# Moving weight loads around the last cross-attention section of a fused decoder kernel

## Chip, core and metric

The kernel runs on one core of one Trainium2 chip. The metric is device time in microseconds (us) of one launch, as the median of several runs. The kernel before the change has a median of 1155.73 us over three runs (1155.29 to 1156.04).

## The reference, cut to what matters

Sixteen sequences of 128 rows and 512 columns go through one decoder layer and then through a gated cross-attention layer, all in float32.

```python
# decoder layer
x = x + attention(layernorm(x, ln1) @ w_qkv + b_qkv, ltor_mask) @ w_ao + b_ao          # self attention, 16 heads of 32
x = x + attention(layernorm(x, ln2) @ w_q + b_q, ctx @ w_kv + b_kv, cross_mask) @ w_co + b_co
x = x + gelu(layernorm(x, ln3) @ w1 + b1) @ w2 + b2                                     # 512 -> 2048 -> 512
# gated layer: keys and values come from the same ctx
a = layernorm(ctx, gamma, beta)
x = x + tanh(gate) * (attention(x @ Wq.T, a @ Wk.T, a @ Wv.T, mask) @ Wo.T)
```

## The kernel before

**Sections and steps.** The sixteen sequences form four groups of four. The decoder's attention is eight sections in a row: A0 to A3 (self attention of each group) and B0 to B3 (cross attention of each group). A section has sixteen steps, numbered 0 to 15, four for each sequence (called a batch here); the last section, B3, is followed by eight steps of run-out, numbered 16 to 23. In every step the function `attend` lets each engine do a little of several pipelines: the scores of a batch at steps 0, 4, 8 and 12; the exponentials, sums and scaling of one unit (four heads) per step; and what other sections need later. The order of all instructions is written out by hand and kept (`keep_in_program_order`). Each engine works through its own list in that order.

**How probabilities reach TensorE.** After scaling, a unit's probabilities are transposed on VectorE and stored to DRAM (`away_B <- s_B`, 256 KB). Two units later they are fetched as a pair in four parts (`pT_B <- away_B`, 4 x 128 KB) into one of three `pT` buffers. Then TensorE mixes them with the values (`av_B <- pT_B, v_B`) and projects (`mo_B`). For B3 the pairs are fetched at steps 7 and 9 for the first batch (mixed at step 12), 11 and 13 for the second (step 15), 14 and 16 for the third (step 18), 18 and 20 for the fourth (step 22).

**One queue for transfers.** Nearly all DMAs are issued by SyncE (SP in the profile) in the written order. They use eight semaphores in turn, so a DMA cannot be issued before the one eight places ahead of it has landed.

**What else runs beside B2 and B3.** While B2 runs, `FirstGated.prepare` normalizes the gated layer's first group (`back_a`, `T_a`) and loads the transposed key weight `w_gk` in steps 8 to 11 and the value weight `w_gv` in steps 12 to 15, in four parts of 256 KB each; they were written to DRAM much earlier. While B3 runs, `beside_last_cross` projects that group's keys (steps 1, 2, 3, 5) and values (7, 9, 13, 15) and prepares the MLP: it normalizes group 0 and sends it turned through DRAM (`turned_C`, then `back_C`, four parts at steps 7, 7, 9, 9), and it fetches rows of `x` that lay in DRAM (`x <- kept_x_B`, steps 1, 1, 3).

**The MLP.** It is a generator (`mlp`) that is advanced by one `piece` at the listed steps. It works in sixteen stages n of seven rounds r; stage 0 begins at step 17 of B3. Stage n needs a block of w1 and a block of w2 (1 MB each, `w1_n` and `w2_n`, both plainly `w` in the profile) and sums of their quarters (`t`). In the first group the sums are stored to DRAM for reuse (`kept <- t`, 1 MB each). The parts of `w1_0` are loaded in steps 12 to 15 of B2. The eight 256 KB parts of `w2_0` and then `w1_1` are queued in `ml.pieces` and issued at the steps in `loads`. In stage 0 VectorE takes two jobs per round from `todo`: the sums of `w2_0` (`first`), then those of `w1_1` and the store of these (`more`). The sums of `w1_0` are stored at the end of round 3.

The rounds fall on the steps as follows: n = 0 has r = 0 at step 17, r = 1 at 18, r = 2 and 3 at 19, r = 4 at 20, r = 5 and 6 at 21; n = 1 begins at step 22. A `piece` begins with `due()`, which issues what the pieces before it left for later, such as a store.

**Weight buffers.** All weights share six buffers (`wpool`, tag `w`). A new tile takes a buffer that is free by the written order, and its load waits until the last reader of the old tile is done.

Of the kernel before, what the change touches and what calls it, by code (L numbers as in the profile page):

```python
# [16 lines left out]
P = 128  # L17
# [3 lines left out]
NQ = S // Q  # L21
# [33 lines left out]
def decoder_then_gated_cross_attention(ctx: ExitStack, tc: tile.TileContext, a: dict, out: bass.AP):  # L55
# [945 lines left out]
    class CrossAttention(Section):  # L1001
# [34 lines left out]
        def jobs(self):  # L1036
            g, n, lnT, encT = self.g, self.name, self.lnT, self.encT
            mask = work.tile([P, 2, GB, S], F32, tag="mask", name=f"mask_{g}", bufs=2)
            self.ms, self.ma = mask[:, 0], mask[:, 1]
            nc.sync.dma_start(  # L1040
                out=self.ms, in_=a["mask_Bx1xSxS2_ff1"][g * GB : (g + 1) * GB, 0].rearrange("b q k -> q b k")
            )
            qkv_tiles(self)
            tokens_at = [x[g][:, b].rearrange("p (o t) -> p o t", t=HF) for b in range(3)]
            token_sides, sums = right_blocks(encT, tokens_at)
            if g == 0:
                self.begin()
            products = [
                block_product(halves(self.k), self.k_sides, token_sides, False, f"k_{n}", ("b_k", 0)),
                block_product(by_quarters(self.v), self.v_sides, token_sides, True, f"v_{n}"),  # L1050
            ]
            return plan(
                ([lambda c=c: self.query_chunk(c) for c in range(KC)], [0, 1, 3, 5]),
                *blocks_plan(products, CROSS_BLOCKS if g else FIRST_CROSS_BLOCKS), ([lambda: mask_terms(self.ms, self.ma)], [7]),
                ([lambda o=o: nc.gpsimd.tensor_tensor(*o) for o in sums], [0, 1, 2, 3]),
                *(self.weights_begin() if g == 0 else decoder[NG + g - 1].tokens_again([5, 9, 13])),
            )

        def query_chunk(self, c):
# [81 lines left out]
    def mlp_start(ml):  # L1141

        ml.b2 = load_row(a["L0_xattn_b2"], "b2_row")
        ml.db1 = cpool.tile([P, NF], F32, tag="db1", name="db1")
        for i in range(NI):
            b1, c0 = columns["b1"]
            c0 += i * KC
            nc.vector.tensor_tensor(
                ml.db1[:, 2 * i : 2 * i + 2], b1[:, c0 + 2 : c0 + 4], b1[:, c0 : c0 + 2], ALU.subtract
            )  # L1150

        def row_difference():
            ml.db2 = work.tile([P, H], F32, tag="row", name="db2_row", bufs=2)
            nc.vector.tensor_tensor(ml.db2[:, 0:HF], ml.b2[:, HF:H], ml.b2[:, 0:HF], ALU.subtract)

        ml.lnT = []
        def start():
            ml.lnT.append(act_tile("C0"))
            ml_begin(0)

        sends = [lambda b=b: ml_send(0, b) for b in range(GB)]
        back = [lambda k=k: chunk_back(ml.lnT[0][:, k], ml.back, k, "ln3_s", "ln3_b") for k in range(KC)]
        return (
            ([start, row_difference, lambda: ml_receive(0)], [0, 5, 7]), (sends, [0, 1, 2, 3]), (back, [12, 13, 14, 14]),
            ([lambda m=m: ml.part(m) for m in range(NQ)], [7, 7, 9, 9])
        )

    def ml_begin(g):
# [8 lines left out]
    def mlp(ml, last_steps):  # L1177
# [145 lines left out]

        w1[0] = load(0, 1)
        yield
        w2[0], w1[1] = load(0, 2), load(1, 1)
        right1[0], todo, _ = sums(0, 1, "enc", w1.pop(0), nc.gpsimd)
        yield
        for do in todo:
# [7 lines left out]
        for n in range(len(steps) + 1):  # L1337
            todo, more = deque(), []
            at_ = {r: [] for r in range(7)}
            h = lnT = None  # L1340
            if n + 1 < len(steps):
                right1[n + 1], more, back = sums(n + 1, 1, "v", w1.pop(n + 1))
                at_[3].append(back)
            if n < len(steps):
                g, i = steps[n]
                right2[n], first, back = sums(n, 2, "enc", w2.pop(n))
                todo.extend(first + more)
                at_[4].append(back)
                h = work.tile([P, KC, TG], F32, tag="qT", name=f"h_{n}", bufs=2)
                if i == 0 and n:  # L1350
                    sides = following
                if g + 1 < NG and i == 1:
                    at_[0].append(lambda: ml_begin(g + 1))
                    for b in range(GB):
                        at_[b].append(lambda b=b: ml_send(g + 1, b))
                elif g + 1 < NG and i == 2:
                    lnT = turned_tile(g + 1)
                    at_[0].append(lambda: ml_receive(g + 1))
                    for m in range(NQ):
                        at_[m // 2].append(lambda m=m: ml.part(m))  # L1360
                    for c in range(KC):
                        at_[3 + c].append(
                            lambda c=c: chunk_back(lnT[c // 2][:, c % 2], ml.back, c, "ln3_s", "ln3_b")
                        )
                    next_lnT = lnT
                elif g + 1 < NG and i == 3:
                    following, more = sums_of(g + 1, next_lnT)
                    for r, do in enumerate(more):
                        at_[3 + r].append(do)
            if before is not None:  # L1370
                for r, do in enumerate(before[1]):
                    at_[r].append(do)
            for r in range(7):
                if n < len(steps):
                    p = H_ORDER[r]
                    hidden_product(n, p, sides[p], right1[n][p], h)
                if before is not None:
                    p = O_ORDER[r]
                    out_product(n - 1, p, before[0][p], right2[n - 1][p], acc)
                for _ in range(min(2, len(todo))):  # L1380
                    todo.popleft()()
                for do in at_[r]:
                    if do is not None:
                        do()
                if r == 1 and n + 1 < len(steps):
                    w2[n + 1] = load(n + 1, 2)
                elif r == 2 and n + 2 < len(steps):
                    w1[n + 2] = load(n + 2, 1)
                last_steps(n, r)
                if (n, r) in ((0, 3), (1, 3)):  # L1390
                    d, t = unkept.pop(0)
                    nc.sync.dma_start(out=d, in_=t)
                yield
            if n < len(steps):
                t = work.tile([P, 3, 2, HF], F32, tag="kT", name=f"sh_{n}", bufs=2)
                before = token_sums(halves(h), t[:, 0], t[:, 1], t[:, 2])
# [59 lines left out]

    class FirstGated:


        def prepare(self, p):  # L1460
            if p == 0:
                self.raw = work.tile([P, GB, H], F32, tag="enc", name="enc_D0", bufs=2)
                self.ln, self.away = ln_tile("D0"), away_tile("D0")
            if p in (0, 1):
                for b in (2 * p, 2 * p + 1):
                    nc.sync.dma_start(out=self.raw[:, b, :], in_=a["ctx_2048"][b])
            elif p >= 2 * GB:
                key, k = ("gk", "gv")[p // GB - 2], p % GB
                if k == 0:
                    w[key] = wpool.tile([P, KC, H], F32, tag="w", name=f"w_{key}")  # L1470
                nc.sync.dma_start(out=w[key][:, k], in_=gated[key][:, k])
            if 2 <= p < 6:
                q = p - 2
                normalize_and_send(self.raw[:, q, :], self.ln[:, q], self.away, "D0", q)
            if p >= 12:
                if p == 12:
                    next(in_mlp)
                ml.pieces.popleft()()
            if p in (9, 11):
                if p == 9:  # L1480
                    self.back, self.part = receiver("a0", self.away)
                for m in range(2):
                    self.part(m + 2 * (p == 11))
            if p >= 12:
                if p == 12:
                    self.aT = act_tile("a0", "enc")
                group_back(self.aT, self.back, "gamma", "beta", [p - 12])
# [232 lines left out]
    def beside_last_cross():  # L1720
        flip[0], in_blocks[0] = 2, False
        def piece():
# [1 line left out]
            next(in_mlp)  # L1724

        at_ = [2, 3, 4, 5, 6, 15, 15, 16, 16, 17, 18, 19, 19, 20, 21, 21, 22, 23, 23]
        loads = [5, 7, 9, 11, 13, 14, 15, 16]
        return plan(
            *gated_start(first), *mlp_start(ml), *decoder[-1].tokens_again([1, 1, 3], (1, 0, 2)), ([piece] * len(at_), at_),
            ([lambda: ml.pieces.popleft()()] * len(loads), loads),  # L1730
        )

# [94 lines left out]
```

## Time and profile before

| what | value |
|---|---|
| median of 3 runs | 1155.73 us |
| the profiled execution's own time | 1154.62 us |
| its span (first to last instruction) | 1152.8 us |
| TensorE (PE) busy in the span | 1129.9 us |
| mean granted TensorE clock | 0.997 |
| DMA traffic | 259.81 MB, mean 225 GB/s |
| DMA busy share and rate, 443 to 477 us | 1.04, 277 GB/s |
| the same, 508 to 531 us | 0.99, 269 GB/s |
| scores of B3's batches (`sc_B`), start | 465.34, 481.38, 494.00, 506.35 us |
| first MLP product (`h`), start | 519.88 us |

Every instruction is recorded under one line, L51, which is the helper that keeps the order, so rows are told apart by their tiles: `out <- in`. Buffer numbers are left out, so `w` is any block of w1 or w2 and `t` any of their sums. The scores mark the steps: step 0 of B3 begins at about 465 us, step 4 at 481, step 8 at 494, step 12 at 502 (its mix comes ahead of the scores), step 16 at 519. An idle time in brackets stands before an instruction with the releaser that ended it. The granted clock is the share of full speed that TensorE was given. SP rows are issues of DMAs; the transfer itself runs later.

### The profile page before, as it was taken

The page shows a single profiled execution, that of the slowest core. Times are in us where ns is not written, and L with a number is a line of the kernel's source. Part 1 is how long each engine was busy: PE and PEld are TensorE (multiplying, and loading weights), DVE is VectorE, ACT ScalarE, POOL GpSimd, SP SyncE. Part 2 cuts the span into 40 slices and gives each one's busy share as a digit, 9 for nine tenths or more (in the row PEclk, how much of TensorE's full clock was granted, in tenths as well). Part 3 has the DMA queues.
Part 4 walks back from the last instruction along what each step waited for, and adds up shares of the span by engine and source line. Part 5 has one row for each costly group of instructions (what it writes and reads, how often), then busy time and mean ns, then how long its engine had stood idle before and what let it go on. Part 6 is the DMA issues. An engine that isn't in the chain of part 4 may idle for free.

```text
span 1152.8 us, 22191 instructions
## 1 busy us (share of the span) xinstructions
PE 1129.9 (98%) x7246; PEld 873.1 (76%) x7246; DVE 743.4 (64%) x1919; ACT 611.1 (53%) x2142; POOL 694.6 (60%) x633
## 2 busy tenths in 40 slices
PE   9999999999999999999999999999999999999998
PEld 8877777666675757546788888888888877878875
DVE  6678978798787776987564634443342237767754
ACT  3567676767667666774231333233222337877663
POOL 6798888788868685773333414443342168545873
PEclk9999999999999999999999999999999999999999
DMA  6588889999888879999696696697447827888975
GB/s 222 159 211 233 217 221 224 256 240 260 210 225 217 233 217 250 289 285 294 226 258 234 183 283 191 201 274 261 155 154 228 261 59 201 236 253 230 267 220 175
DMA packets 325284, 259.81 MB, mean 225 GB/s; under 512 B 83560, under 2 KB 280624, under 8 KB 320304
## 3 DMA queue, kind: packets, MB, share of 16 engines
q1 hardware_dynamic: 325128, 258.38, 78.8%
q8 instruction: 58, 0.95, 0.4%
q14 instruction: 58, 0.48, 0.1%
q10 hardware_dynamic: 40, 0.01, 0.0%
HBM read 163.94 MB, written 94.37 MB: 224 GB/s over the span
## 4 chain that ended last, share of the span: by engine, by line
PE 71%; DMA 10%; POOL 6%; DVE 5%; ACT 3%; issue 3%; SPq 2%; POOLq 0%; DVEq 0%; ACTq 0%
PE h L51 17%; PE o L51 16%; PE mo_A L51 4%; PE mm_q_B L51 3%; PE mm_v_B L51 3%; PE mo_B L51 3%; PE mm_v_A L51 3%; PE mm_q_A L51 3%; PE mm_v_D L51 3%; PE mm_k_A L51 3%; PE mm_k_B L51 3%; PE mm_q_D L51 2%; DMA away_D<-s_D 2%; POOL x L51 2%; SPq L51 2%
## 5 line engine op out<-in xcount | busy, mean ns | idle before, releaser
L51 DVE TENSOR_TENSOR h<-h,h 128x512 f32<-128x512 f32 x80 | 54.9, 686 | 114.5 <-PE h L51 114.5
L51 ACT ACTIVATE h<-h 128x512 f32<-128x512 f32 x64 | 40.3, 630 | 161.5 <-DVE h L51 161.5
L51 ACT ACTIVATE s_A<-s_A,mn_A 128x128 f32<-128x128 f32 x256 | 99.4, 391 | 46.7 <-issue 24.1
L51 ACT ACTIVATE s_B<-s_B,mn_B 128x128 f32<-128x128 f32 x256 | 99.4, 392 | 31.1 <-issue 18.2
L51 POOL TENSOR_TENSOR s_D<-s_D,sum_D 128x512 f32<-128x512 f32 x64 | 66.5, 1040 | 57.7 <-DVE sum_D L51 52.2
L51 ACT ACTIVATE s_D<-s_D,mn_D 128x128 f32<-128x128 f32 x256 | 99.1, 392 | 0.4 <-issue 0.4
L51 POOL TENSOR_TENSOR s_B<-s_B,sum_B 128x512 f32<-128x512 f32 x64 | 67.1, 1048 | 52.2 <-DVE sum_B L51 38.1
L51 POOL TENSOR_TENSOR s_A<-s_A,sum_A 128x512 f32<-128x512 f32 x64 | 66.7, 1042 | 30.5 <-DVE sum_A L51 23.9
L51 POOL TENSOR_TENSOR s_A<-s_A,ma 128x512 f32<-128x512 f32 x64 | 81.9, 1280 | 5.1 <-DVE s_A L51 4.1
L51 POOL TENSOR_TENSOR s_B<-s_B,mask 128x512 f32<-128x512 f32 x60 | 76.6, 1277 | 2.2 <-DVE s_B L51 1.3
L51 POOL TENSOR_TENSOR rstd_aD<-rstd_aD,mhalf 128x1 f32<-128x1 f32 x12 | 6.6, 550 | 115.1 <-DVE rstd_aD L51 101.6
L51 POOL TENSOR_TENSOR sh<-h 128x512 f32<-128x512 f32 x32 | 40.6, 1270 | 50.6 <-ACT h L51 49.6
L51 PE MATMUL h<-sx,t 128*128 128x256 f32 x256 | 61.9, 386 | 2.0 <-ACT h L51 2.0
L51 PE MATMUL h<-T_C,w 128*128 128x256 f32 x256 | 61.1, 381 | 0.8 <-DVE h L51 0.8
L51 PE MATMUL h<-T_C,t 128*128 128x256 f32 x256 | 60.6, 379 | 1.0 <-DVE h L51 1.0
L51 PE MATMUL o<-w,h 128*128 128x256 f32 x256 | 60.9, 381 | 0.0
L51 PE MATMUL o<-t,h 128*128 128x256 f32 x256 | 60.5, 379 | 0.0
L51 PE MATMUL o<-t,sh 128*128 128x256 f32 x256 | 60.5, 379 | 0.0
L51 DVE CUSTOM_DVE_ANT_0 s_D<-sc_D,gmask 128x128 f32<-128x128 f32 x256 | 57.2, 283 | 2.1 <-DMA turned_x<-x_D 1.2
L51 PE MATMUL mo_B<-w_co,mT_B 128*128 128x512 f32 x128 | 57.6, 593 | 0.0
L51 PE MATMUL mo_A<-w_ao,mT_A 128*128 128x512 f32 x128 | 57.5, 592 | 0.0
L51 PE MATMUL mm_q_B<-T_B,w_cq 128*128 128x512 f32 x128 | 57.4, 596 | 0.0
(335 smaller groups left out, 3002.0 us busy)
## 6 DMA issues: line engine op xcount, KB each, us to landing
t<-kept SPq DMA_DIRECT2D x24, 1024.0 KB, 8.0
away_A<-s_A SPq DMA_DIRECT2D x64, 256.0 KB, 3.1
pT_A<-away_A SPq DMA_DIRECT2D x128, 128.0 KB, 3.5
away_B<-s_B SPq DMA_DIRECT2D x64, 256.0 KB, 4.5
pT_B<-away_B SPq DMA_DIRECT2D x128, 128.0 KB, 3.7
away_D<-s_D SPq DMA_DIRECT2D x60, 256.0 KB, 3.5
pT_D<-away_D SPq DMA_DIRECT2D x120, 128.0 KB, 2.7
w<-in_L_xattn_w_dram SPq DMA_DIRECT2D x24, 512.0 KB, 6.1
```

Of the source, the lines that this page charges most:

```text
L51: return lambda *args, **kw: self.tc.keep_in_program_order(call(*args, **kw))
```

## The change

- `w_gk` is loaded in steps 14, 14, 15, 15 of B1 in place of steps 8 to 11 of B2; `w_gv` in steps 6 to 9 of B2 in place of 12 to 15.
- `w1_1` comes before `w2_0` in the queue of parts: its parts are issued in steps 2, 3, 4, 5 of B3, those of `w2_0` in steps 13, 15, 16, 17. Before, `w2_0` went at 5, 7, 9, 11 and `w1_1` at 13, 14, 15, 16.
- In stage 0 of the MLP the sums of `w1_1`, with their store, come ahead of those of `w2_0`.
- The last two parts of `back_C` are fetched at step 8 in place of 9; the three rows of `x` at steps 2, 4, 5 in place of 1, 1, 3.

```diff
@@ CrossAttention.jobs
                 *(self.weights_begin() if g == 0 else decoder[NG + g - 1].tokens_again([5, 9, 13])),
+                *(
+                    [([lambda k=k: first.fetch_weight_part("gk", k) for k in range(KC)], [14, 14, 15, 15])]
+                    if g == 2 else []
+                ),
@@ mlp_start
-            ([lambda m=m: ml.part(m) for m in range(NQ)], [7, 7, 9, 9])
+            ([lambda m=m: ml.part(m) for m in range(NQ)], [7, 7, 8, 8])
@@ mlp
-        w2[0], w1[1] = load(0, 2), load(1, 1)
+        w1[1], w2[0] = load(1, 1), load(0, 2)
...
-                todo.extend(first + more)
+                todo.extend(first + more if n else more + first)
@@ FirstGated
+        def fetch_weight_part(self, key, k):
+            if k == 0:
+                w[key] = wpool.tile([P, KC, H], F32, tag="w", name=f"w_{key}")
+            nc.sync.dma_start(out=w[key][:, k], in_=gated[key][:, k])
...
-            elif p >= 2 * GB:
-                key, k = ("gk", "gv")[p // GB - 2], p % GB
-                if k == 0:
-                    w[key] = wpool.tile([P, KC, H], F32, tag="w", name=f"w_{key}")
-                nc.sync.dma_start(out=w[key][:, k], in_=gated[key][:, k])
+            elif 6 <= p < 10:
+                self.fetch_weight_part("gv", p - 6)
@@ beside_last_cross
-        loads = [5, 7, 9, 11, 13, 14, 15, 16]
+        loads = [2, 3, 4, 5, 13, 15, 16, 17]
...
-            *gated_start(first), *mlp_start(ml), *decoder[-1].tokens_again([1, 1, 3], (1, 0, 2)), ([piece] * len(at_), at_),
+            *gated_start(first), *mlp_start(ml), *decoder[-1].tokens_again([2, 4, 5]), ([piece] * len(at_), at_),
```

## The prediction, made before the changed kernel was run

> **What bounds the kernel now.** I read the first part of the page, then who waited for whom on TensorE around B3, its timeline there, the clock in single stretches, and last SP's issues.
>
> ```profile
> PE 1129.9 (98%) x7246; PEld 873.1 (76%) x7246; DVE 743.4 (64%) x1919; ACT 611.1 (53%) x2142; POOL 694.6 (60%) x633
> ```
>
> TensorE is the bound. A change of load times can only act on its idle time, 22.9 us in all, and on the slow stretches behind it. From 400 to 570 us, around everything that the change moves, TensorE waited for this:
>
> ```profile
> PE av_B L51 <- DMA pT_B<-away_B: 2.5, 2, 1.9
> PE h L51 <- ACT h L51: 2.0, 1, 2.0
> PE h L51 <- DVE h L51: 1.8, 2, 1.0
> PE mm_k_B L51 <- ACT q_B L51: 0.6, 1, 0.6
> ```
>
> Only the first row hangs on a transfer: the mixes of steps 12 and 18 waited for fetched probabilities. The `h` rows are the MLP's chain through ACT and DVE.
>
> ```profile
> 504.71 1.71 PE L51 MATMUL av_B<-pT_B,v_B 128*32 128x128 f32 x28 [1.91 <-DMA pT_B<-away_B]
> 506.35 2.09 PE L51 MATMUL sc_B<-k_B,q_B 32*128 32x128 f32 x32
> ...
> 528.00 1.07 PE L51 MATMUL av_B<-pT_B,v_B 128*32 128x128 f32 x28 [0.63 <-DMA pT_B<-away_B]
> ...
> 543.95 1.89 PE L51 MATMUL o<-w,h 128*128 128x256 f32 x8
> 545.77 1.08 PE L51 MATMUL av_B<-pT_B,v_B 128*32 128x128 f32 x32
> 548.84 3.32 PE L51 MATMUL h<-sx,t 128*128 128x256 f32 x8 [1.99 <-ACT h L51]
> ```
>
> The 1.91 us cost more than themselves. Undisturbed, 32 mixes take 1.01 us to the next instruction (480.37 to 481.38) and 32 scores 1.11 (to 482.49). Here 28 mixes took 1.64, which is 0.76 over 28/32 of 1.01, and the scores 2.02, 0.91 over. So this wait is worth 1.91 + 0.76 + 0.91 = 3.6 us. The mix of step 22, at 545.77, did not wait.
>
> ```profile
> 504.70:508.40 3.70, 3.69 (x61) 3.09 (x61) 2.98 (x6) 2.83 (x15) 3.30 (x4) 0.54 1.10 296
> 548.80:552.00 3.20, 3.16 (x9) 2.53 (x10) 2.48 (x4) 0.69 (x1) 0.00 (x0) 0.59 0.25 70
> 565.00:569.00 4.00, 3.44 (x16) 3.05 (x17) 2.72 (x5) 1.65 (x3) 0.93 (x1) 1.00 1.05 354
> ```
>
> The last three columns are granted clock, DMA share and GB/s. After idle times of 1.91 and 1.99 us the clock was 0.54 and 0.59; after 0.98 us (before 565.56) it stayed 1.00.
>
> ```profile
> 494.01 0.91 SPq L51 DMA_DIRECT2D back_C<-turned_C  x2
> 495.25 0.36 SPq L51 DMA_DIRECT2D w<-in_L_xattn_w_dram  x1
> 495.73 1.96 SPq L51 DMA_DIRECT2D away_B<-s_B  x2
> 497.78 2.13 SPq L51 DMA_DIRECT2D pT_B<-away_B  x4
> 500.78 1.02 SPq L51 DMA_DIRECT2D back_C<-turned_C  x2
> ...
> 532.44 0.51 SPq L51 DMA_DIRECT2D w<-in_L_xattn_w_dram  x1
> 532.99 1.16 SPq L51 DMA_DIRECT2D kept<-t  x1
> 538.36 2.21 SPq L51 DMA_DIRECT2D pT_B<-away_B  x4
> 540.66 0.44 SPq L51 DMA_DIRECT2D kept<-t  x1
> ```
>
> Two places to see. The fetch of step 9 (497.78) has two `back_C` parts and one weight part ahead of it and two `back_C` parts behind. The fetch of step 20 (538.36) has one 1 MB store ahead of it and the store of the `w1_1` sums (540.66) behind.
>
> The landing records of the trace show that transfers line up: they land in the order of issue. At step 9 the fetch's last part landed at 504.58, 0.13 us ahead of its mix. At step 20 the landings were `w1_2` 540.86, `kept` 543.47, the fetch's last part 545.59. TensorE was free for that mix at 545.77, so the slack was 545.77 - 545.59 - 0.13 = 0.05 us.
>
> **The change, part by part.**
>
> *Gated weights sooner.* 1 MB each leaves steps 8 to 11 and 12 to 15 of B2. Buffers are free: `w_ao` is last read in A3's projections, before 294 us, and `w_cq` at 426.87 us, before step 6. Where they go, pairs land 7 us or more ahead of their mixes (the fetch of step 5 in B2 ends its issue at 423.3 for a mix at 433.85), which covers four parts at some 0.75 us each; uncovered it would be 3 us. What is gained: at step 12 of B2, ACT waited 1.29 us for `back_a` (455.97), and DVE, busy without a break from 458.4 to 480.9, and POOL, busy without one from 480.9 to 497.5, stood behind it. So the probabilities of step 9 leave up to 1.3 us sooner.
>
> *`w1_1` and `x` rows.* By the landings, a 256 KB transfer takes some 0.7 us of the line. After 477 us, when transfers landed in 2.4 to 2.9 us and nothing stood in line, and ahead of the fetch of step 9, stood two weight parts (steps 5 and 7) and one row (3). Now three parts (3, 4, 5) and two rows (4, 5) stand there: one of each more, 1.4 us.
>
> *`back_C` at 8.* Two parts more ahead of the same fetch. The pair at 500.78 added 2.3 us to the line (505.01 to 507.28). Nothing waited for `back_C` at step 12 (no such row in ACT's waits), so its earlier landing gains nothing.
>
> Sum at step 12: 1.4 + 2.3 - 1.3 = +2.4 us if the line was full from 477 us on. It moved 292 GB/s from 477 to 495 us and 331 from 531 to 546, so 39 GB/s x 18 us = 0.70 MB, or 2.1 us at 331 GB/s, may have been spare. Small packets do not reach that rate; I take two thirds, 1.4. That leaves **+1.0 us**, bounds -3.6 (the wait gone) and +2.4.
>
> *Step 18.* Its fetch loses the weight part of step 14, which had landed before. I take **-0.2**, bounds -0.6 (the wait gone) and +0.7 (one part more).
>
> *Order in stage 0.* TensorE needs neither block's sums before stage 1, so the sums cost nothing by themselves; if `w2_0` landed too late, DVE would wait up to 0.7 us for its last part. But the store of `w1_1`'s sums moves with them. Before, it was the ninth job, taken in round 4 (step 20) and issued at step 21, behind the fetch of step 20. Now it is the fifth, taken in round 2 and issued by the second `piece` of step 19, ahead of the other store and of the fetch. 1 MB took 2.6 us of the line (540.86 to 543.47). The fetch lands 2.6 us later, slack 0.05, so the mix of step 22 waits 2.55. At half clock its 32 matmuls take 0.76 x 32/28 = 0.87 more. Behind it wait ACT's `mT_B`, then ACT's `h`, then TensorE at 548.84, whose slow stretch was there before. Together **+3.4 us**. Below: 0, if the line has room. Above: one more weight part (step 17), 0.7, and 1 MB at 331 GB/s, 3.2: 2.55 + 0.6 + 0.7 + 0.9 = 4.8. DVE waits too: its sums at 543.49 waited for the first store's landing (1.4 us), now 2.6 us later; that runs beside the same delay.
>
> [...]
>
> Sum: 1.0 - 0.2 + 3.4 = +4.2 us. The profiled execution took 1154.62 us around a span of 1152.8; it becomes 1158.8. The median of the runs is 1.11 above it: 1155.73 + 4.2 = **1159.9**.
>
> **Rivals.**
>
> *The line has room, faster.* Transfers overlap instead of lining up, at 531 us as at 497, so neither the parts nor the store push the fetches back, and the 2 MB that left B2 let the fetch of step 9 come in time. Then 3.6 + 0.6 go and nothing comes: 1151.5. For it: latency was down to 2.4 us near 477 us. Against: landings in order, a share near 1. It decides from the point where the last part of step 9 lands 1.9 us sooner and the 1 MB costs the fetch of step 20 under 0.3 us.
>
> *Both, no change.* The first wait goes (-3.6, -0.2) and the store's wait comes (+3.4): 1155.3. For it: the 1.3 us and the spare rate at their best.
>
> *All in a full line.* +2.4 + 0.7 + 4.8 = +7.9: 1163.6; the upper end of my own case.
>
> That the loads do not really come sooner would need a buffer or data held; both are free, as shown.
>
> **How the numbers follow.** A measurement of this kernel tells 0.2% (2.3 us) from no change. My case, slower, has 0.60, from 1158.1 (the store's wait without its clock, 2.55 - 0.2) to 1163.0; no change 0.19; faster 0.21, since ACT, busy without a break from 508.6 to 517.6, would eat part of that gain: 1151.5 to 1153.4. The range leaves out half of the faster case and the tip of mine: 1152.5 to 1162.8.
>
> **What would show it.** Right: a wait of some 2.5 us before the mix of step 22 on `pT_B <- away_B`, with a clock near 0.55 behind it; two `kept <- t` issues in a row ahead of a fetch; the wait of step 12 still there, 2 to 4 us. Wrong: no wait at step 22, or none at step 12, or a new one at steps 0 to 8 of B2, where the gated loads now stand.

## The result, and the profile after

Measured beside the kernel before on the same chip, the changed kernel took 1161.55 us (median of 8 runs, 1158.16 to 1165.94) against 1155.51 (8 runs, 1154.23 to 1158.61): a ratio of 1.0056 [1.0040, 1.0072]. It is slower, by about 6 us. The forecast was 1159.9, slower, with a range that ends at 1162.8. The profiled execution took 1161.65 us around a span of 1159.9, so the two profiled spans lie 7.1 us apart (1159.9 - 1152.8).

The page of the changed kernel, the row of busy times:

```profile
PE 1131.9 (98%) x7246; PEld 873.8 (75%) x7246; DVE 742.8 (64%) x1919; ACT 612.1 (53%) x2142; POOL 694.4 (60%) x633
```

Of the 7.1 us, 2.0 are longer work on TensorE (1131.9 against 1129.9: the same instructions, more of them at half speed). The other 5.1 are idle time. Where it lies, the waits of TensorE from 400 to 580 us say (us in total, times, longest):

```profile
PE av_B L51 <- DMA pT_B<-away_B: 7.3, 4, 5.0
PE h L51 <- ACT h L51: 2.0, 1, 2.0
PE h L51 <- DVE h L51: 1.8, 2, 1.0
PE mm_k_B L51 <- ACT q_B L51: 0.6, 1, 0.6
```

Three rows are those of before. The first grew from 2.5 us in two waits to 7.3 in four, 4.8 more: nearly all of the added idle time is waiting for fetched probabilities. The timeline of TensorE after the change shows the four (start, duration, instruction, idle time before it):

```profile
493.85 1.07 PE L51 MATMUL av_B<-pT_B,v_B 128*32 128x128 f32 x28 [0.18 <-DMA pT_B<-away_B]
508.47 1.92 PE L51 MATMUL av_B<-pT_B,v_B 128*32 128x128 f32 x28 [5.05 <-DMA pT_B<-away_B]
510.32 2.09 PE L51 MATMUL sc_B<-k_B,q_B 32*128 32x128 f32 x32
...
532.14 1.07 PE L51 MATMUL av_B<-pT_B,v_B 128*32 128x128 f32 x28 [0.26 <-DMA pT_B<-away_B]
...
552.09 1.07 PE L51 MATMUL av_B<-pT_B,v_B 128*32 128x128 f32 x28 [1.77 <-DMA pT_B<-away_B]
555.12 3.78 PE L51 MATMUL h<-sx,t 128*128 128x256 f32 x8 [1.96 <-ACT h L51]
```

The same places as shifts against before, from the starts of like instructions in the two timelines:

| from ... to | added there, us | forecast |
|---|---|---|
| start to the scores of step 0 (465.34, now 465.60) | +0.26 | 0 |
| to the scores of step 8 (494.00, now 494.84) | +0.58 | 0 |
| step 12, wait and slow clock | +3.67 | +1.0 |
| step 18 | -0.37 | -0.2 |
| step 22, wait and slow clock | +3.47 | +3.4 |
| from there to the end | -0.5 | 0 |

Steps 18 and 22 came near the size worked out. Step 12 came out at more than three times its size, and a small wait at step 8 was not foreseen.

The issues of SP after the change, around the fetch of step 9 (499.82) and around that of step 20 (541.86):

```profile
495.08 1.68 SPq L51 DMA_DIRECT2D back_C<-turned_C  x2
497.62 0.38 SPq L51 DMA_DIRECT2D away_B<-s_B  x1
498.37 0.80 SPq L51 DMA_DIRECT2D back_C<-turned_C  x2
499.34 0.38 SPq L51 DMA_DIRECT2D away_B<-s_B  x1
499.82 2.66 SPq L51 DMA_DIRECT2D pT_B<-away_B  x4
...
536.17 0.51 SPq L51 DMA_DIRECT2D w<-in_L_xattn_w_dram  x1
536.72 1.59 SPq L51 DMA_DIRECT2D kept<-t  x2
541.86 2.20 SPq L51 DMA_DIRECT2D pT_B<-away_B  x4
```

Four parts of `back_C` now stand ahead of the fetch of step 9, and two stores of 1 MB (`kept<-t x2`) ahead of that of step 20. The fetch of step 9 is issued 2.0 us later than before (497.78). What SP waited for from 494 to 500 us (us in total, times, longest), first before the change:

```profile
SPq L51 <- DVE s_B L51: 1.2, 1, 1.2
SPq L51 <- DMA back_C<-turned_C: 0.2, 1, 0.2
```

Then after it:

```profile
SPq L51 <- DMA away_B<-s_B: 1.3, 2, 1.0
SPq L51 <- DMA kept_k_D<-k_D: 0.8, 1, 0.8
SPq L51 <- ACT mT_B L51: 0.4, 1, 0.4
```

Before, SP waited mostly for the probabilities that VectorE makes (DVE); now it waits mostly for earlier transfers to land. In the traces of the two kernels all transfers that SP issued after 100 us (1012 before, 1013 after) landed in the order of issue, and never more than eight were under way. The landing records of the changed kernel's trace give the price of what was moved: the two early parts of `back_C` took 2.2 us of the line (from the landing ahead of them at 502.91 to 505.13), and the second store took 2.55 us (547.26 to 549.81). The last part of the fetch of step 20 landed at 551.96, 0.13 us ahead of its mix.

### The profile page after: what moved, and what is told of

It is laid out like the page before. It is cut to its first block, busy times and chain, and to the rows that moved or that the text cites. A ratio compares the mean times of both kernels' runs of the same rounds, so it can differ in the third digit from the quotient of the medians.

```text
span 1159.9 us, 22182 instructions
## 1 busy us (share of the span) xinstructions
PE 1131.9 (98%) x7246; PEld 873.8 (75%) x7246; DVE 742.8 (64%) x1919; ACT 612.1 (53%) x2142; POOL 694.4 (60%) x633
## 4 chain that ended last, share of the span: by engine, by line
PE 64%; DMA 6%; DVE 5%; POOL 4%; issue 1%; ACT 1%; SPq 1%; POOLq 0%; DVEq 0%; ACTq 0%
PE o L51 16%; PE h L51 16%; PE mm_v_D L51 4%; PE mm_v_B L51 3%; PE mm_k_B L51 3%; PE mm_q_D L51 3%; PE mm_q_B L51 3%; PE mo_B L51 3%; PE mm_k_D L51 2%; DMA pT_B<-away_B 2%; PE mm_o_D L51 2%; PE mo_A L51 1%; PE sc_B L51 1%; PE av_D L51 1%; PE sc_D L51 1%
```

## The experiments

Experiments begin either from the changed kernel, with one part taken back, or from the kernel before, with one part or one suspected cost added. In each trace the wait ahead of a mix is read from TensorE's timeline. The table has all of them (waits in us ahead of the mixes; the ratio is to the kernel before in the same comparison, whose median there was 1154.8 to 1156.3). The ratios are estimates with a 95% interval and not quotients of the medians, which differ from them by up to 0.16 points.

| kernel | step 8 | step 12 | step 18 | step 22 | median, us | ratio to before |
|---|---|---|---|---|---|---|
| before | 0 | 1.91 | 0.63 | 0 | 1155.51 | 1 |
| before, profiled again | 0 | 1.36 | 1.95 | 0 | 1154.8 | - |
| after | 0.18 | 5.05 | 0.26 | 1.77 | 1161.55 | 1.0056 [1.0040, 1.0072] |
| after, store behind | 0.99 | 3.66 | 0.68 | 0.55 | 1159.38 | 1.0017 [0.9998, 1.0036] |
| after, `back_C` at 9 | 1.35 | 1.79 | 0.23 | 3.30 | 1161.38 | 1.0040 [1.0022, 1.0058] |
| after, both of these | 1.54 | 2.76 | 0 | 0 | 1155.68 | 1.0004 [0.9985, 1.0023] |
| after, blocks back | 0 | 4.09 | 0 | 1.28 | 1159.35 | 1.0014 [0.9993, 1.0034] |
| after, rows back | 1.07 | 3.36 | 0 | 2.01 | 1162.08 | 1.0053 [1.0034, 1.0072] |
| before, gated sooner | 0 | 0.52 | 0.97 | 0 | 1154.77 | 0.9980 [0.9963, 0.9997] |
| before, a second store | 0 | 1.84 | 2.38 | 3.04 | 1158.81 | 1.0019 [1.0002, 1.0036] |
| before, tiny transfers | 0.39 | 2.77 | 2.71 | 0 | 1157.24 | 1.0019 [0.9997, 1.0041] |
| before, gated sooner, two parts | 0 | 1.06 | 1.05 | 0 | 1153.47 | 0.9977 [0.9962, 0.9993] |
| before, gated sooner, six parts | 0 | 0 | 0.88 | 0.67 | 1154.27 | 0.9989 [0.9970, 1.0007] |

The waits are those of one profiled execution each. How far one such number can be trusted, the kernel before shows, profiled a second time with nothing edited:

> The kernel before, profiled a second time, to see how far a wait differs between two executions of one program. Theory (the line's timetable decides, and single loads from DRAM differ by 1 to 2 us in landing): the wait at step 12 lies within 1.2 us of 1.91, that at step 18 within 1.2 of 0.63, and that at step 22 under 1.2. Rival (waits repeat, so that differences of a few tenths between kernels count): all three within 0.3 us of the first profile.

```profile
503.65 1.07 PE L51 MATMUL av_B<-pT_B,v_B 128*32 128x128 f32 x28 [1.36 <-DMA pT_B<-away_B]
527.90 1.16 PE L51 MATMUL av_B<-pT_B,v_B 128*32 128x128 f32 x28 [1.95 <-DMA pT_B<-away_B]
```

Where the first execution had 1.91 and 0.63, this one has 1.36 and 1.95. A wait differed by up to 1.3 us between two executions of one program, slightly more than the 1.2 expected, so single differences below 1.3 us are read here only where several kernels repeat them. The loads differ by as much: of the 338 that the two kernels issue alike from 30 to 392 us, 14 differed by over 1 us in their time from issue to landing between the two profiled executions, 1.57 us at most.

**Is the wait of step 22 the store's?** First from the changed kernel: the jobs of `w1_1` stay ahead of those of `w2_0`, the store alone goes behind.

```diff
-                todo.extend(first + more if n else more + first)
+                todo.extend(first + more if n else more[:-1] + first + more[-1:])
```

> The changed kernel with one thing taken back: in stage 0 the store of the w1_1 sums is again the last of the nine jobs, so it is issued at step 21, behind the fetch of step 20. The order of the sums stays changed. Theory (transfers stand in one full line, and 1 MB ahead of the fetch costs the mix of step 22): the wait of 1.77 us before the mix of step 22 goes to under 0.3, the wait of 5.05 at step 12 stays at 4.5 to 5.5, and the time falls by 3.5 us to about 1158. Rival (the wait at step 22 comes from the parts of w2_0 that now go at steps 13 to 17, or from probabilities that leave late): the wait at step 22 stays over 1.2 us and the time within 1 us of 1161.5.

SP's issues and TensorE's mix in this kernel:

```profile
536.54 2.23 SPq L51 DMA_DIRECT2D kept<-t  x1
544.02 1.81 SPq L51 DMA_DIRECT2D pT_B<-away_B  x4
545.87 0.43 SPq L51 DMA_DIRECT2D kept<-t  x1
```

```profile
550.51 1.07 PE L51 MATMUL av_B<-pT_B,v_B 128*32 128x128 f32 x28 [0.55 <-DMA pT_B<-away_B]
```

One store ahead of the fetch and one behind it, as before: the wait is down from 1.77 to 0.55 us (under 0.3 was expected), the excess from 0.56% to 0.17%, and the wait of step 12 fell too, to 3.66, which was not expected. So most of the wait came with the store and not with the order of the sums, which is still the changed one here.

Then the same cost put into the kernel before. It stores the first sums a second time into a scrap tensor, right behind the first store, and changes nothing else:

```diff
+                    if n == 0:
+                        again = dram.tile([P, 4, 2, HF], F32, tag="again", name="again")
+                        nc.sync.dma_start(out=again, in_=t)
```

> The kernel before, in which the first store (the sums of w1_0, 1 MB) is followed by a second one of the same data to another place in DRAM, both ahead of the fetch of step 20; nothing reads the second. Theory (full line): the fetch lands 2.6 us later against the issue of the w2_1 load, and the mix of step 22, which did not wait, waits 2 to 3 us; with the clock lost behind it the time rises by 2.5 to 4 us to about 1159. Rival (the new wait of the changed kernel came from something else that moved with the order of sums): no wait over 1 us at step 22 and the time within 1 us of before.

```profile
533.62 2.08 SPq L51 DMA_DIRECT2D kept<-t  x1
535.75 0.60 SPq L51 DMA_DIRECT2D again<-t  x1
541.15 1.90 SPq L51 DMA_DIRECT2D pT_B<-away_B  x4
```

```profile
550.09 1.07 PE L51 MATMUL av_B<-pT_B,v_B 128*32 128x128 f32 x28 [3.04 <-DMA pT_B<-away_B]
```

A wait of 3.04 us appears where there was none, in a kernel that has no other part of the change. The time rose by 0.2 to 4.2 us (the interval of the ratio; the medians lie 4.0 apart), so it is not settled whether the wait costs more or less than itself. The four kernels with 1 MB more ahead of this fetch waited 1.77, 3.30, 2.01 and 3.04 us, 2.53 on average; the forecast priced the wait at 2.55. By the landing records of these four traces the extra store landed 2.45 to 2.55 us behind the store ahead of it; the waits differ more, since TensorE was ready for the mix 5.5 and 5.6 us after the weight load ahead of both stores had landed where it waited 1.77 and 2.01, and 3.4 us after where it waited 3.30 and 3.04. In the nine other executions of the table it is 0 six times, and 0.55, 0.67 and 1.28.

**What makes the wait of step 12?** Three parts of the change push the fetch of step 9 back: `back_C`, the blocks and the rows of `x`. The gated weights act against them. `back_C` first:

```diff
-            ([lambda m=m: ml.part(m) for m in range(NQ)], [7, 7, 8, 8])
+            ([lambda m=m: ml.part(m) for m in range(NQ)], [7, 7, 9, 9])
```

> The changed kernel with the last two parts of back_C fetched at step 9 again, behind the fetch of the probabilities. Theory (full line): the two parts leave the line ahead of that fetch, 2.3 us by the landings in the kernel before, so the wait at step 12 falls from 5.05 to 2.4 to 3.2 us, the wait at step 22 stays near 1.8, and the time falls by 2 to 3 us to about 1159. Rival (the weight parts and rows of x at steps 2 to 5 made the fetch late, back_C had room): the wait at step 12 stays over 4.3 us and the time near 1161.5.

```profile
505.50 1.07 PE L51 MATMUL av_B<-pT_B,v_B 128*32 128x128 f32 x28 [1.79 <-DMA pT_B<-away_B]
...
548.32 1.07 PE L51 MATMUL av_B<-pT_B,v_B 128*32 128x128 f32 x28 [3.30 <-DMA pT_B<-away_B]
```

The wait of step 12 fell from 5.05 to 1.79, but that of step 22 rose from 1.77 to 3.30, and the median moved by no more than the intervals allow. The first is lower than expected (2.4 to 3.2); the second (1.8 expected) and the time (2 to 3 us less expected) were missed. In these two executions TensorE was ready for the mix of step 22 at 545.02 (548.32 - 3.30) instead of 550.32, 5.3 us sooner, but the mix began only 3.8 us sooner, as its fetch landed only 3.8 us sooner (548.18 instead of 551.96): the transfers ahead of it set its time, and who arrives sooner waits longer for it. Time won at the first place can only be kept if the second is mended too, which the next kernel does (both edits at once):

> The changed kernel with two things taken back: the store of the w1_1 sums behind the fetch of step 20, and the last two parts of back_C at step 9. The gated weights, the two weight blocks and the rows of x stay changed. Theory (full line): the wait at step 12 is about 1.8 us as without the early back_C alone, the wait at step 22 is under 1.2 us in place of 3.3, and the time is 1156 to 1157.5, about as before the change. Rival (the blocks' new places cost most by themselves): the wait at step 22 stays over 2 us and the time over 1159.

It has waits of 1.54, 2.76 (1.8 expected), 0 and 0, and a ratio of 1.0004 [0.9985, 1.0023]. The two small edits take nearly the whole loss back, and what then remains of the change is worth nothing that can be measured.

The parts of the two blocks next, put back to the old steps and the old order, with the old order of sums:

```diff
-        w1[1], w2[0] = load(1, 1), load(0, 2)
+        w2[0], w1[1] = load(0, 2), load(1, 1)
...
-                todo.extend(first + more if n else more + first)
+                todo.extend(first + more)
...
-        loads = [2, 3, 4, 5, 13, 15, 16, 17]
+        loads = [5, 7, 9, 11, 13, 14, 15, 16]
```

> The changed kernel with the two weight blocks back in their old order and places (w2_0 at 5, 7, 9, 11, w1_1 at 13 to 16) and with the old order of sums and store; the gated weights, back_C at 8 and the rows at 2, 4, 5 stay changed. Theory (full line): two parts of back_C (2.3 us) and one row (0.75) more than before ahead of the fetch of step 9, 1 us less from the probabilities that leave sooner: the wait at step 12 is 1.9 + 2.3 + 0.75 - 1.0 = 3.9 us, none at step 22, the time about 1158. Rival (w1_1 in steps 2 to 5 is what made the line long): the wait at step 12 is under 2 us and the time at or under 1155.5.

The wait of step 8 is gone (0.18 to 0), that of step 12 was 4.09 (3.9 expected): the early blocks are not what makes most of it. The wait of 1.28 at step 22, with the store in its old place, was not expected. It is of the size of the spread, and its cause stays open. The rows of `x` put back to steps 1, 1 and 3:

```diff
-            *gated_start(first), *mlp_start(ml), *decoder[-1].tokens_again([2, 4, 5]), ([piece] * len(at_), at_),
+            *gated_start(first), *mlp_start(ml), *decoder[-1].tokens_again([1, 1, 3], (1, 0, 2)), ([piece] * len(at_), at_),
```

> The changed kernel with the three rows of x fetched at steps 1, 1, 3 again. Theory (full line): two 256 KB transfers go from the busy steps 4 and 5 to step 1, where the line is empty, so the fetches of steps 5 and 9 land up to 1.4 us sooner: no wait at step 8, 3.5 to 4.5 us at step 12 in place of 5.05, time 1159.5 to 1161. Rival (rows are out of the way at steps 4 and 5): waits as in the changed kernel, time within 0.7 us of 1161.5.

It waited 1.07 us at step 8, where none was expected, and 3.36 at step 12 (3.5 to 4.5 expected), and took the same time as the changed kernel (1.0053 [1.0034, 1.0072]). The rows decide nothing that a run can tell.

Do the early blocks hurt by their bytes, or by their places in a queue that had at most eight transfers under way? The kernel before got four transfers of 512 bytes at step 8, into a tile that nothing reads:

```diff
+        def tiny(n):
+            nc.sync.dma_start(out=scrap[n : n + 1, :], in_=a["L0_xattn_b2"][n * P : (n + 1) * P].rearrange("(c p) -> c p", p=P))
...
-            ([lambda: ml.pieces.popleft()()] * len(loads), loads),
+            ([lambda: ml.pieces.popleft()()] * len(loads), loads), ([lambda n=n: tiny(n) for n in range(4)], [8] * 4),
```

> The kernel before with four more transfers of 512 bytes each at step 8 of B3, ahead of the fetch of step 9, into a tile that nothing reads: four places among the eight transfers that may be under way, and nearly no bytes. Theory (bytes stand in line): the wait at step 12 changes by less than 0.7 us from 1.91 and the time by less than 1. Rival (the limit of eight transfers under way holds SP back, so that each transfer more costs, whatever its size): the fetch's parts wait for back_C parts to land before they are issued, the wait at step 12 rises by 1.5 us or more, and the time by 1.5 to 3 us.

SP's issues in it:

```profile
499.39 2.08 SPq L51 DMA_DIRECT2D scrap<-in_L_xattn_b_dram  x4
502.50 0.39 SPq L51 DMA_DIRECT2D away_B<-s_B  x1
503.38 2.29 SPq L51 DMA_DIRECT2D pT_B<-away_B  x4
```

With 2 KB in all they hold SP for 2.08 us, and the fetch of step 9 begins at 503.38 instead of 497.78. Of these 5.6 us, however, 2.3 were there at step 8 already (its scores start at 496.33 instead of 494.00). The wait of 2.77 is only 0.9 to 1.4 above that of the two profiles of before. This lies between both theories and inside the spread: places and bytes are not separated.

**What does the part that should help bring?** The gated weights sooner, alone, in the kernel before:

```diff
+                *(
+                    [([lambda k=k: first.fetch_weight_part("gk", k) for k in range(KC)], [14, 14, 15, 15])]
+                    if g == 2 else []
+                ),
...
-            elif p >= 2 * GB:
...
+            elif 6 <= p < 10:
+                self.fetch_weight_part("gv", p - 6)
```

> The kernel before with one part of the change alone: w_gk at steps 14, 14, 15, 15 of B1 and w_gv at steps 6 to 9 of B2. Theory: ACT's wait for back_a at step 12 of B2 goes, POOL's unbroken stretch begins about 1 us sooner, and the wait at step 12 of B3 falls from 1.91 to about 0.9 us; an idle time that short leaves the clock at 1.00, so 1.0 + 1.7 = 2.7 us are gained, about 1152.8. Rival (TensorE runs ahead of ACT and DVE, and waits later instead): the waits at steps 15, 18 and 22 grow by 1 to 2 us together and the time is 1154 to 1155.5.

```profile
503.19 1.07 PE L51 MATMUL av_B<-pT_B,v_B 128*32 128x128 f32 x28 [0.52 <-DMA pT_B<-away_B]
523.24 1.99 PE L51 MATMUL h<-sx,t 128*128 128x256 f32 x8 [1.00 <-POOL sx L51]
526.55 1.07 PE L51 MATMUL av_B<-pT_B,v_B 128*32 128x128 f32 x28 [0.97 <-DMA pT_B<-away_B]
```

A ratio of 0.9980 [0.9963, 0.9997]: this part by itself makes the kernel slightly faster, narrowly clear of no change (the medians lie 1.5 us apart; 2.7 were expected). The wait of step 12 is down to 0.52 us. TensorE then waits 1.00 us for `sx` from POOL, which it does in the second profile of before too (0.93). Over the stretch from 460 to 580 us the granted clock was 1.00, where it was 0.97 in the first profile of before.

Can steps 2 and 3, where nothing stands in line, take two parts of the first block, with the order of the blocks kept?

```diff
-        loads = [5, 7, 9, 11, 13, 14, 15, 16]
+        loads = [2, 3, 10, 11, 13, 14, 15, 16]
```

> The gated weights sooner as in the kernel with that part alone, and the two weight parts that stood ahead of the fetch of step 9 moved away from it: the parts of w2_0 at steps 2, 3, 10, 11 in place of 5, 7, 9, 11; everything else as before the change. Theory (full line): two 256 KB parts less in the busy stretch ahead of the fetch, up to 1.4 us, so no wait at step 12 where 0.5 was left, and the time at or under that of the gated weights alone, 1153 to 1154.5. Rival (two parts at steps 2 and 3 push the fetch of step 5 as the four did): a wait of 0.5 us or more at step 8, and the time at or over 1155.

```profile
503.00 1.07 PE L51 MATMUL av_B<-pT_B,v_B 128*32 128x128 f32 x28 [1.06 <-DMA pT_B<-away_B]
```

It took 1153.47 us, 0.9977 [0.9962, 0.9993], which is not told apart from the gated weights alone. There is no wait at step 8, so the two parts did no harm there; but a wait of 1.06 at step 12, where none was expected, shows no gain from moving them. Moving the other parts forward too, out of the way of the later fetches, brought no more:

```diff
-        loads = [5, 7, 9, 11, 13, 14, 15, 16]
+        loads = [2, 3, 10, 11, 12, 13, 13, 14]
```

> The gated weights sooner, the parts of w2_0 at steps 2, 3, 10, 11 and those of w1_1 at 12, 13, 13, 14 in place of 13 to 16, so that none stands at steps 15 and 16 ahead of the fetches of steps 16 and 18. Theory (full line): the wait of about 1 us at step 18 goes or halves, 0.5 to 1 us gained over the kernel with parts at 2, 3, 10, 11 alone: 1152 to 1153.5. Rival (1 MB in steps 10 to 13 pushes the fetch of step 13): a wait at step 15, and a time over 1154.

The wait of step 12 was 0, those of steps 18 and 22 were 0.88 and 0.67, and the ratio was 0.9989 [0.9970, 1.0007]. The wait of step 18 that this edit was to remove stayed (1.05 to 0.88).

## Why the prediction was right or wrong

**Direction and time: right**, with the main mechanism. Four fifths of the forecast +4.2 were the store ahead of the fetch of step 20, and this was shown from both sides: put back, it lowered the ratio from 1.0056 to 1.0017 (intervals just apart); added to the kernel before, it made that 0.19% slower [0.02%, 0.36%] with a wait of 3.04 us. The landing records show the priced 2.6 us of the line as 2.55. The two issues `kept<-t` in a row were there as forecast.

**Step 22, +3.4: right in size, wrong in how it is made up.** Measured +3.47, from a wait of 1.77 (forecast 2.55; the store took that time of the line, but four mixes ran first, 0.4 us, and the rest is smaller than the spread) and a longer time at half clock. The forecast put 0.87 us of slow clock on the mix itself. That mix ran at full speed, 1.07 us; the loss came behind it, at 555 to 561 us, where the slow stretch now lasts twice as long (6.83 us from 554.42, against 3.41 from 549.35 before). The agreement of the sum is therefore partly luck, and the price by wait, "worth 3.6", is no price that carries over (see the last section). The lower end of the slower case, 1158.1, took the store's wait without its clock; in the profiled execution the clock fell at 554.42, behind the wait of 1.77 us and within the next one, of 1.96.

**Step 12, +1.0: the step that failed is the two terms that were to hold the wait down**: the discount for spare rate, "I take two thirds, 1.4", and the -1.3 for probabilities that leave sooner. Of what pushes the fetch back, the two parts of `back_C` were priced well, at +2.3: the two kernels with them early beside all the rest wait 4.36 (5.05, 3.66), the two with them at 9 wait 2.28 (1.79, 2.76): +2.1, and the landing records say 2.2. The weight part and the row were priced at 0.7 each; without the one the wait was 4.09, without the other 3.36, so 0.3 and 1.0, both inside the spread. The part of step 2 was not counted; it was issued at 477.82, after the 477 us from which the prediction counts. The three kernels whose transfers ahead of step 9 are the old ones wait 1.70 on average (1.91, 1.36, 1.84), so up to the 4.36 the wait grew by 2.7 where +1.0 was forecast. Now the two terms that were to hold it down.

The -1.3 for the gated weights fits the one execution where they are moved alone: the wait is 0.52 there, 1.2 less. In the changed kernel the last transpose on VectorE ahead of the fetch does begin 0.71 us sooner. Before:

```profile
496.54 0.71 DVE L51 STREAM_TRANSPOSE s_B<-s_B 128x512 f32<-128x512 f32 x1 [0.31 <-POOL s_B L51]
```

After:

```profile
495.83 0.71 DVE L51 STREAM_TRANSPOSE s_B<-s_B 128x512 f32<-128x512 f32 x1 [0.31 <-POOL s_B L51]
```

But the store of these probabilities, the last one ahead of the fetch, is issued at 499.34, 2.0 us later than before (497.32), since SP first issues the `back_C` parts and waits for earlier transfers to land. The time won does not reach the fetch.

The discount came from a mean rate over 18 us, and the spare rate was hardly there. These are the stretches of the changed kernel (PE, PEld, DVE, ACT, POOL busy, granted clock, DMA share, GB/s):

```profile
443.00:477.00 34.00, 34.00 (x226) 21.85 (x225) 26.49 (x60) 22.72 (x84) 19.99 (x20) 1.00 0.84 224
477.00:495.00 18.00, 17.82 (x133) 8.73 (x135) 14.67 (x30) 11.40 (x48) 16.99 (x16) 1.00 1.04 303
```

From 477 to 495 us the rate rose only from 292 to 303 GB/s, 0.2 MB in 18 us, where 0.47 MB (two thirds of 0.70) had been counted on. That small packets do not reach 331 GB/s is in the packet records of the kernel before: from 477 to 495 us those of 512 and 1024 bytes, 69% of the bytes, moved 291 and 275 GB/s (16 engines, over the packets' own time); those of 8 KB moved 408 from 531 to 546 us. Even the two thirds that were left for this were not spare. The 2 MB taken out of B2 show in the stretch ahead of it: share 0.84 and 224 GB/s from 443 to 477 us, where before it was 1.04 and 277. The room that was made lies ahead of the place that needed it. In the profiled pair the wait grew by 3.14, beyond the forecast's upper bound of +2.4, and mainly by half clock that lasted longer it became the +3.67 of the table. How much of the error belongs to each of the two terms is open: without the discount alone the sum is +2.4, without the -1.3 alone +2.3, without both +3.7, and all three lie closer to 2.7 than the spread of 1.3.

**The chain of the gated weights: right.** The activation of ACT that waited 1.29 us for `back_a` no longer waits, and POOL's unbroken stretch begins at 480.22 instead of 480.95: 0.73 us sooner, or 1.0 against TensorE, which is 0.26 later there, of the 1.3 forecast. What became of it is said above.

```profile
454.91 0.81 ACT L51 ACTIVATE T_a<-back_a,vcols 128x512 f32<-128x512 f32 x1
```

```profile
480.22 0.55 POOL L51 TENSOR_TENSOR rstd_C<-rstd_C,mhalf 128x1 f32<-128x1 f32 x1 [1.01 <-DVE rstd_C L51]
```

**Step 18, -0.2: right in sign** (0.63 to 0.26), but below the spread.

**What was left out: the fetches of the batch before.** Parts at steps 2 to 5 stand in line ahead of the pair that is mixed just before the scores of step 8. All five kernels with these parts there wait 0.18 to 1.54 us (1.03 on average); of the eight others only the one with tiny transfers does (0.39). The prediction asked only what stands ahead of the fetch of step 9.

**The rivals.** *The line has room* fell: no wait went away in the changed kernel. *Both, no change* fell with it. *All in a full line* (1163.6) was right about the line at step 12, and too high for steps 18 (+0.7 against -0.37) and 22 (+4.8 against +3.47).

## What to carry to other kernels

SP's queue landed its transfers in the order of issue here, at a share of 1.04 from 477 to 495 us and 0.92 from 531 to 546 in the changed kernel. In it a load that nobody waits for cost the time that the next just-in-time fetch behind it waited. So for every moved transfer list the fetches that it now precedes, those of earlier steps too. When jobs are reordered, look at what travels with them; here a store, whose result TensorE does not read, made TensorE wait 2.5 us on average for the fetch behind it. Time won by an engine ahead of a transfer is kept only if the queue can issue sooner too: here the last transpose began 0.71 us sooner and the store was issued 2.0 us later. A mean rate below the highest one seen (292 against 331 GB/s) was no sign of room here: it rose by less than half of what had been counted on (0.2 of 0.47 MB).

## What the runs showed of the hardware

The granted clock did not follow single waits. In the traces of the kernel before and of the changed kernel its records change only at points that lie a multiple of 3.41 us apart within a run: it fell at 504.98 and 549.35 us before, 13 times 3.41 apart, and at 506.63 and 554.42 in the changed kernel, 14 times. The time between two such points that lie 3.41 us apart is called a unit here. The next two fences cut the run at these points (second number: TensorE busy; third from the right: clock). The changed kernel:

```profile
503.22:506.63 3.41, 0.20 (x4) 0.00 (x0) 3.03 (x6) 2.00 (x10) 3.01 (x3) 1.00 1.10 318
506.63:510.04 3.41, 1.57 (x28) 1.36 (x28) 1.50 (x3) 1.35 (x8) 2.50 (x3) 0.50 0.93 280
510.04:513.46 3.42, 3.42 (x38) 2.40 (x35) 0.99 (x4) 2.96 (x12) 0.00 (x0) 0.50 1.07 326
...
551.01:554.42 3.41, 1.07 (x28) 0.83 (x28) 1.39 (x5) 1.22 (x5) 1.78 (x2) 1.00 0.55 60
554.42:557.83 3.41, 2.71 (x6) 2.19 (x7) 2.03 (x4) 1.35 (x3) 0.00 (x0) 0.50 0.10 28
557.83:561.25 3.42, 3.42 (x9) 2.70 (x8) 3.11 (x7) 0.81 (x1) 1.79 (x2) 0.50 0.95 290
```

The kernel before, profiled again:

```profile
525.34:528.75 3.41, 1.46 (x34) 0.97 (x32) 2.48 (x5) 0.00 (x0) 2.39 (x2) 1.00 0.71 195
528.75:532.16 3.41, 3.41 (x15) 2.51 (x9) 3.38 (x6) 1.14 (x4) 0.00 (x0) 0.50 0.55 164
...
545.82:549.23 3.41, 2.57 (x40) 1.84 (x38) 0.33 (x2) 0.77 (x4) 1.79 (x2) 1.00 0.89 226
549.23:552.64 3.41, 2.26 (x10) 2.01 (x11) 1.58 (x3) 1.80 (x5) 0.00 (x0) 1.00 0.00 0
```

A unit in which TensorE was idle for 1.95 us (3.41 - 1.46) was followed by half clock. A wait of 1.99 us, from 548.39 to 550.38, that a border cut into 0.84 and 1.15 cost no clock at all; in the first execution of the same program the wait at the same place, also 1.99 us (546.85 to 548.84), fell into one unit (545.94 to 549.35) and brought half clock. At step 22 of the changed kernel two waits, neither over 1.96 us, added up to 2.34 idle in one unit, and the drop came at its end. Half clock lasted one unit where that held no idle time (504.98 and 549.35 before, 528.75 in its second profile), and two where the first held 0.70 us or more (1.84 at 506.63, 0.70 at 554.42). By these numbers, as an estimate, a drop costs 1.7 us in a unit full of work (half of 3.41). In the traces of the kernel before and of the changed one the units at full clock ahead of a drop had 1.91, 1.99, 2.34 and 3.21 us of idle time; of the units behind which the clock stayed at 1.00, the one with the most had 1.73 before (1129.62 to 1133.03) and 1.80 after (1155.17 to 1158.58).

So the same wait of 1.99 us cost no clock in one execution and a unit at half clock in another; by the estimate above it is worth 2.0 us in the one and 3.7 in the other, by where it falls on the grid of these points. The grid did not go with the work: in three kernels that are the same up to step 8 of B3 (before, a second store, tiny transfers) its points lay 3.2, 1.6 and 0.5 us behind a multiple of 3.41 us from the first instruction. Much of the spread of one kernel went with the clock. The fastest and the slowest run of the changed kernel (1158.16 and 1165.94) had a mean granted clock of 0.997 and 0.992, and 0.005 of 1160 us is 5.8 of the 7.8 us between them. Of 31 runs of the kernel before in one comparison, the 13 with a mean clock of 1.000 have a median of 1153.4 us, the 11 with 0.998 or 0.999 one of 1155.1, and the 7 with 0.997 or less one of 1158.9.
